# Graph-network stack on one core: job results of the pair stage added in twos by GpSimd ahead of the product with the identity

## Chip, core and metric

The kernel runs on one core of one Trainium2 chip. The metric is the time on the device in microseconds, lower is better; it is given as the median of several executions. TensorE (PE), its weight loads (PEld), VectorE (DVE), ScalarE (ACT), GpSimd (POOL) and the DMA queues (SyncE's is SP) work from queues of their own, in order, and wait for each other by semaphores.

## The reference

The reference is a stack of four graph layers over 2048 nodes, 8 batches and 64 features, each added to its input after a layer norm and a relu. The change lies in layer 0. Its part that matters here is this, with H the 2048 x 64 membership of nodes in hyperedges:

```python
all_he = beta[..., None] * h[:, None, :, :] + (1.0 - beta[..., None]) * agg[:, :, None, :]
all_he = jax.nn.elu(all_he)
...
coefs1 = jax.nn.softmax(logits2, axis=-1)
g = jnp.einsum('bne,benf->bnf', coefs1, all_he)
...
industry = jnp.einsum('nm,bmf->bnf', adj / deg, x @ W_ind)
```

For each node n, g sums over the hyperedges e that hold the node: elu of a mixture of the node's own features h and the hyperedge's features agg, weighted by coefs1. A node is in few hyperedges, so the kernel walks only over the pairs that exist. The industry term is a dense product with the adjacency matrix.

## The kernel before, in words

The kernel first tests on the chip whether the short form applies; with these inputs it does. The nodes are then ordered by the number of hyperedges that they are in, and cut into 16 tiles of 128 nodes. HELD (line 35) says for each j how many tiles hold nodes with more than j hyperedges. From it the class Pairs makes its list of jobs, (tile t, slot j): 57 in all, 12 for tile 0, 5 for tiles 1 and 2, 4 for tiles 3 to 5, 3 for tiles 6 to 9, 2 for tiles 10 to 14, and 1 for tile 15. Each job works on a block of 128 nodes x 512 values (8 batches x 64 features) in fp32.

The stage runs inside layer0_pairs. The dense product for the industry term, adj_product (line 321), loops over 4 column chunks and 16 row tiles: in each of these 64 steps it casts a block of the adjacency matrix on ScalarE (line 344) and issues 8 products, four with x_ind_hi and four with x_ind_lo, into four accumulators named pp. After each step it calls `after`, which runs one `Pairs.step()` and one piece of a side job, the naming of lists (line 2462). That side job has a VectorE comparison (L2469), 13 small products and a copy (L2478), each of them once in four steps. At the end of a chunk, VectorE multiplies the four accumulators into their place (L872).

One call of `Pairs.step()` works on four jobs in different states, as a software pipeline:

- job i: VectorE subtracts the gathered hyperedge row pa (in PSUM) from the node's row h (L2335), GpSimd scales the difference by beta (L2324, called from `scale`);
- job i-1: VectorE adds pa back (L2339), ScalarE makes exp(-relu(-d)) in two instructions (L2341, L2342);
- `gather(i + 1)`: two products of the selection matrix `pick` with agg_hi and agg_lo into a pa bank, of which there are two; if the job opens a new tile, first the fetch of a later tile by an indirect DMA on GpSimd's queue (L2268) and the tile's set-up (lines 2273 to 2309: `pick` on VectorE, small pb products, beta and coef);
- job i-2: VectorE forms y = max(d, 0) + e (L2347), GpSimd scales y by coef (L2324);
- job i-3: TensorE adds y to the tile's accumulator acc as a product with the identity (in fp32, two recorded matmuls each, `kern.mm` at line 177); at the tile's last job ScalarE writes the accumulator minus one (L2359), and a DMA on SyncE's queue stores it to g_rows.

d, e and y are rings of 8, 6 and 8 buffers; two further places of e hold the results for storing. All of TensorE's `kern.mm` products have line 177 in the profile. The stage behind it (`mix`) gathers g_rows by indirect DMAs (L890); none of these can start before all g_rows are stored.

The order in each engine's queue is not the order in which the program lists the instructions. A scheduler puts them in order when the kernel is built, from its own estimates of cost and readiness. It keeps dependences, but it may put VectorE's instructions of neighbouring jobs in another order than `step` lists them. Only three instructions in a later stage are told to keep program order.

Of the kernel before, what the change touches and what calls it, by code (L numbers as in the profile page):

```python
# [7 lines left out]
F = mybir.dt.float32  # L8
# [4 lines left out]
AF = mybir.ActivationFunctionType  # L13
# [6 lines left out]
P = 128  # L20
# [6 lines left out]
CW = 512  # L27
# [108 lines left out]
class Kernel:  # L136
# [184 lines left out]
    def adj_product(self, src, w, ps, done, each=None, first=None, after=None, bufs=4, step=2, casts=None):  # L321
# [4 lines left out]
        for ch in range(NC):  # L326
            out = [ps.tile([P, CW], F, name=f"pp{q}", tag=f"pp{q}") for q in range(NP)]
            if first is not None:
                first(ch, out)
            for g in range(NT // step):  # L330
                at = w.tile([P, step, CW], F, name="adj_t", bufs=bufs)
                nc.sync.dma_start(
                    at,
                    self.a["adjT"][g * step * P : (g + 1) * step * P, ch * CW : (ch + 1) * CW]
                    .rearrange("(t p) n -> p t n", p=P),
                )
                for i in range(step):
                    m = g * step + i
                    if each is not None:
                        each(ch, m, at[:, i])  # L340
                    moving = at[:, i]
                    if self.short:
                        moving = w.tile([P, CW], F12, name="adj_12", bufs=casts or bufs)
                        nc.scalar.copy(moving, at[:, i])
                    for j, part in enumerate(src.parts):
                        for q in range(NP):
                            self.mm(
                                out[q], self.exact(part(m)[:, q * P : (q + 1) * P]),
                                moving,
                                start=first is None and m == 0 and j == 0,  # L350
                                stop=m == NT - 1 and j == 1,
                            )
                    if after is not None:
                        after(ch, m, moving)
            done(ch, out)
# [1886 lines left out]
class Pairs:  # L2242
# [85 lines left out]
    def step(self):  # L2328

        nc, n, i = self.nc, len(self.jobs), self.i  # L2330
        self.i += 1
        if i < n:
            t, j = self.jobs[i]
            d = self.d[:, i % 8]
            nc.vector.tensor_sub(d, self.h[:, t % 4, : NB * D], self.pas[i])  # L2335
            self.scale(d, self.tiles[t][1][:, j])
        if 1 <= i < n + 1:
            d, e = self.d[:, (i - 1) % 8], self.e[:, (i - 1) % 6]
            nc.vector.tensor_add(d, d, self.pas.pop(i - 1))  # L2339

            nc.scalar.activation(e, d, AF.Relu, scale=-1.0)  # L2341
            nc.scalar.activation(e, e, AF.Exp, scale=-1.0)  # L2342
        self.gather(i + 1)
        if 2 <= i < n + 2:
            t, j = self.jobs[i - 2]
            d, e, y = self.d[:, (i - 2) % 8], self.e[:, (i - 2) % 6], self.y[:, (i - 2) % 8]
            nc.vector.scalar_tensor_tensor(y, d, 0.0, e, op0=OP.max, op1=OP.add)  # L2347
            self.scale(y, self.tiles[t][2][:, j])
        if 3 <= i < n + 3:
            t, j = self.jobs[i - 3]  # L2350
            if j == 0:
                self.accs[t] = self.ps.tile([P, CW], F, name="acc")
            self.kern.mm(
                self.accs[t], self.kern.ident, self.y[:, (i - 3) % 8], start=j == 0,
                stop=j == self.last[t],
            )
            if j == self.last[t]:
                g = self.e[:, 6 + t % 2]
                nc.scalar.activation(g, self.accs.pop(t), AF.Identity, bias=self.less)  # L2359
                nc.sync.dma_start(self.kern.g_rows[t * P : (t + 1) * P], g)  # L2360

    def end(self):
# [892 lines left out]
```

## Time and profile before

| | us |
|---|---|
| Median of 3 executions | 1943.07 (1941.38 to 1949.31) |
| Profiled execution, its own time | 1993.83 |
| Profiled execution, span | 1992.1 |
| of it, jobs of Pairs (first L2335 to last scaling) | about 214 to 438 |
| of it, end of the dense product (last L872) | 451 |
| TensorE clock granted, mean of the span | 0.918 of full speed |
| GpSimd, L2324, 57 by beta and 57 by coef, in the stage | 76.1 and 63.1 busy |
| ScalarE, casts of the adjacency blocks (L344), 64 | 0.608 each (median) |
| VectorE, naming comparison (L2469), 15 | 2.340 each (median), 1.878 at least |

A row of a group reads: line, engine, operation, output <- inputs by the program's names, shapes, count | busy us, mean ns of one | idle us of the engine just before them, and what ended most of it. The rings and other buffers in the big slots of SBUF all appear as `q`. A row of the waits reads: who waited <- for whom: us in total, times, longest. A row of the timeline reads: start, duration, engine, line, operation, and in brackets how long the engine had been idle before it and what ended that.

### The profile page before, as it was taken

To read this page: it belongs to the slowest core of one execution; us is meant where nothing else is said; L and a number is where in the kernel's file an instruction comes from. 1 tells how busy PE (TensorE), PEld (TensorE's weight loads), DVE (VectorE), ACT (ScalarE), POOL (GpSimd) and SP (SyncE) were. 2 spreads that over 40 slices of the span, in tenths; PEclk is the share of its full clock that TensorE was granted. 3 is DMA by queue.
4 is the path that set the end of the run, shared out by engine and by line. 5 is a ranking of instruction groups with operands and counts; after the bars stand their busy time and mean duration, and the time that the engine had idled before them with its cause. 6 is when DMAs were issued, how large, how long until landed. Compare 5 with 4: busy or idle time off the path is not lost. (4 is left out here: it accounts for less than half of the span.)

```text
span 1992.1 us, 22431 instructions
## 1 busy us (share of the span) xinstructions
PE 1714.6 (86%) x7094; PEld 979.9 (49%) x7098; DVE 1407.7 (71%) x2307; ACT 819.8 (41%) x1650; POOL 1047.7 (53%) x1007
## 2 busy tenths in 40 slices
PE   6888999898888788999999998788787899398884
PEld 2446766663234544444444443466576665244432
DVE  6888788764667787677766566889776675276774
ACT  5722445445566643212120101555555663185300
POOL 1101466668645645776755554563663440767760
PEclk8888999998897997999999998899799898698997
DMA  9641223336436753242220211687677674746555
GB/s 342 262 117 45 75 93 113 103 110 217 127 134 188 238 178 106 64 122 69 74 85 27 88 50 54 218 255 240 201 246 246 190 236 147 249 122 187 169 152 189
DMA packets 127226, 305.22 MB, mean 153 GB/s; under 512 B 29536, under 2 KB 33392, under 8 KB 121968
## 3 DMA queue, kind: packets, MB, share of 16 engines
q0 software_dynamic: 45328, 149.60, 24.8%
q1 hardware_dynamic: 79456, 149.81, 22.2%
q10 hardware_dynamic: 2304, 4.20, 0.6%
q8 instruction: 60, 0.98, 0.2%
q14 instruction: 78, 0.64, 0.1%
HBM read 240.40 MB, written 63.14 MB: 152 GB/s over the span
## 5 line engine op out<-in xcount | busy, mean ns | idle before, releaser
L2615 POOL DMA_INDIRECT raw<-sent,index x300 | 321.3, 1071 | 302.0 <-DVE part_lo L2633 124.6
L2632 ACT CAST part_hi<-raw 128x512 fp32r<-128x512 f32 x352 | 213.0, 619 | 336.0 <-PE acc L177 226.9
L2633 DVE TENSOR_TENSOR part_lo<-raw,part_hi 128x512 fp32r<-128x512 f32 x352 | 264.3, 775 | 113.5 <-ACT part_hi L2632 60.7
L177 PE MATMUL pk<-q,w 128*128 128x512 f32 (+1 forms) x768 | 307.6, 619 | 2.0 <-DVE q L1731 0.9
L1842 POOL TENSOR_TENSOR half<-half,y 128x512 f32<-128x512 f32 x180 | 230.9, 1312 | 117.2 <-DVE y L1835 116.5
L177 PE MATMUL acc<-q,ident 128*128 128x512 f32 x416 | 209.4, 629 | 42.1 <-issue 17.3
L177 PE MATMUL acc<-part_lo,weights 128*128 128x512 f32 x365 | 169.0, 465 | 38.0 <-DVE part_lo L2633 32.2
L177 PE MATMUL acc<-part_hi,weights 128*128 128x512 f32 x365 | 174.4, 481 | 28.4 <-issue 14.1
L177 PEld LDWEIGHTS pk<-q,w 128*128 128x128 f32 (+1 forms) x768 | 117.5, 193 | 156.3 <-issue 121.5
L1835 DVE SCALAR_TENSOR_TENSOR y<-pk,bias,q 128x512 f32<-128x512 f32 x210 | 148.0, 743 | 55.5 <-PE pk L177 37.5
L2944 POOL DMA_INDIRECT ring<-f_rows,near x121 | 138.0, 1141 | 70.2 <-issue 29.9
L177 PEld LDWEIGHTS acc<-q,ident 128*128 128x128 f32 x416 | 78.9, 200 | 121.5 <-issue 70.9
L177 PEld LDWEIGHTS acc<-part_lo,weights 128*128 128x128 f32 x365 | 74.1, 203 | 91.7 <-DVE part_lo L2633 61.4
L2324 POOL TENSOR_TENSOR q<-q,beta 128x512 f32<-128x512 f32 x57 | 76.1, 1337 | 71.3 <-DVE beta L2300 32.9
L177 PEld LDWEIGHTS acc<-part_hi,weights 128*128 128x128 f32 x365 | 73.2, 200 | 79.9 <-issue 49.6
L3015 DVE TENSOR_TENSOR q<-ring,e 128x1024 f32<-128x1024 f32 x58 | 70.1, 1218 | 30.2 <-remote 13.3
L177 PE MATMUL pp<-adj,x_ind_hi 128*128 128x512 f32 x256 | 90.5, 470 | 0.5 <-DVE q L872 0.3
L2601 ACT CAST hub_weights<-dense 128x384 fp32r<-128x384 uint8 x80 | 40.5, 511 | 88.5 <-PE acc L177 84.6
L292 DVE RECIPROCAL std<-std 128x512 f32<-128x512 f32 (+1 forms) x17 | 53.7, 3161 | 30.9 <-ACT std L291 30.9
L2324 POOL TENSOR_TENSOR q<-q,coef 128x512 f32<-128x512 f32 x57 | 63.1, 1108 | 21.2 <-DVE q L2347 16.9
L2532 POOL DMA_INDIRECT listed_raw<-in_adjT_dram,cell x60 | 63.4, 1057 | 16.5 <-issue 16.2
L177 PE MATMUL pp<-adj,x_ind_lo 128*128 128x512 f32 x256 | 72.0, 400 | 0.0
(504 smaller groups left out, 3485.9 us busy)
## 6 DMA issues: line engine op xcount, KB each, us to landing
rows<-in_adj_dram SPq DMA_DIRECT2D x16, 1024.0 KB
adj_t<-in_adjT_dram SPq DMA_DIRECT2D x64, 256.0 KB
own<-sent SPq DMA_DIRECT2D x52, 256.0 KB
raw<-sent SPq DMA_DIRECT2D x52, 256.0 KB
sent<-u SPq DMA_DIRECT2D x48, 256.0 KB
q<-x SPq DMA_DIRECT2D x9, 1024.0 KB
links<-squares POOLq DMA_DIRECT2D x16, 512.0 KB
sent<-q SPq DMA_DIRECT2D x32, 256.0 KB
```

The lines of the kernel that those rows point to most:

```text
L177: self.nc.tensor.matmul(out, lhsT, rhs, start=start, stop=stop)
L292: nc.vector.reciprocal(std, std)
L1835: nc.vector.scalar_tensor_tensor(y, pks[b, half], bias[:, b : b + 1], emb[:, b], op0=OP.add, op1=OP.mult,)
L1842: add.tensor_add(acc, acc, y)
L2324: self.nc.gpsimd.tensor_tensor(x, x, by.unsqueeze(2).to_broadcast([P, NB, D]), op=OP.mult)
L2532: self.kern.behind(nc.gpsimd.indirect_dma_start(raw[:, i], None, rows, bass.IndirectOffsetOnAxis(ap=self.cell[:, c + i : c + i + 1], axis= ...
L2601: self.nc.scalar.copy(to, self.lists.dense[:, :, i * P : (i + 1) * P])
L2615: self.nc.gpsimd.indirect_dma_start(raw, None, self.rows[:], bass.IndirectOffsetOnAxis(ap=self.lists.index[:, c : c + 1], axis=0),)
L2632: nc.scalar.copy(hi, raw)
L2633: nc.vector.tensor_sub(lo, raw, hi.bitcast(F))
L2944: self.nc.gpsimd.indirect_dma_start(to, None, self.kern.f_rows[:], bass.IndirectOffsetOnAxis(ap=index, axis=0))
L3015: nc.vector.tensor_tensor(y.rearrange("n i (b f) -> n i b f", b=NB), block[:, i : i + 2, : NB * D].rearrange("n i (b f) -> n i b f", b=NB) ...
```

## The change

The scaled results y of two neighbouring jobs of one tile are added on GpSimd: for an odd slot j, right after its scaling, y of slot j-1 is added to y of slot j, in place. TensorE then takes only the sums (odd j), and the last y of a tile with an odd number of jobs, into the accumulator. A tile with one or two jobs uses no accumulator: ScalarE reads its y, or its sum of two, directly from SBUF.

```diff
@@ -2346,17 +2346,22 @@
             d, e, y = self.d[:, (i - 2) % 8], self.e[:, (i - 2) % 6], self.y[:, (i - 2) % 8]
             nc.vector.scalar_tensor_tensor(y, d, 0.0, e, op0=OP.max, op1=OP.add)
             self.scale(y, self.tiles[t][2][:, j])
+            if j % 2:
+                nc.gpsimd.tensor_add(y, y, self.y[:, (i - 3) % 8])
         if 3 <= i < n + 3:
             t, j = self.jobs[i - 3]
-            if j == 0:
-                self.accs[t] = self.ps.tile([P, CW], F, name="acc")
-            self.kern.mm(
-                self.accs[t], self.kern.ident, self.y[:, (i - 3) % 8], start=j == 0,
-                stop=j == self.last[t],
-            )
-            if j == self.last[t]:
+            y, last = self.y[:, (i - 3) % 8], self.last[t]
+            if last > 1:
+                if j == 0:
+                    self.accs[t] = self.ps.tile([P, CW], F, name="acc")
+                if j % 2 or j == last:
+                    self.kern.mm(
+                        self.accs[t], self.kern.ident, y, start=j < 2, stop=j == last
+                    )
+            if j == last:
                 g = self.e[:, 6 + t % 2]
-                nc.scalar.activation(g, self.accs.pop(t), AF.Identity, bias=self.less)
+                total = self.accs.pop(t) if last > 1 else y
+                nc.scalar.activation(g, total, AF.Identity, bias=self.less)
                 nc.sync.dma_start(self.kern.g_rows[t * P : (t + 1) * P], g)
```

## Prediction

> **What bounds the kernel now.** I read the page first (engine shares and the 40 slices), then the stage's stretch alone (busy time by window), then who waits for whom in it, then the groups of instructions, and last the timeline of single steps. The page says that TensorE is the busiest engine, but that is a mean over all stages:
>
> ```profile
> span 1992.1 us, 22431 instructions
> PE 1714.6 (86%) x7094; PEld 979.9 (49%) x7098; DVE 1407.7 (71%) x2307; ACT 819.8 (41%) x1650; POOL 1047.7 (53%) x1007
> ```
>
> The jobs of the class Pairs run from the first subtraction at 214.2 us to the last scaling just before 438 us. The stretch 214 to 438 us, columns PE, PEld, DVE, ACT, POOL busy:
>
> ```profile
> 214.00:438.00 224.00, 207.67 (x968) 146.07 (x967) 182.31 (x340) 111.65 (x202) 151.35 (x126) 0.99 0.30 101
> ```
>
> 57 jobs in 224 us are 3.93 us each. TensorE shows 207.7, but ends of matmuls are modelled, so I count it from starts below. Now the waits from 213 to 446 us (total, times, longest):
>
> ```profile
> ...
> POOL q L2324 <- DVE q L2335: 29.4, 26, 2.5
> DVE q L2339 <- POOL q L2324: 28.9, 32, 1.2
> ACT adj L344 <- PE pp L177: 26.3, 20, 3.4
> ...
> PE pa L177 <- DVE q L2339: 12.7, 14, 2.4
> ...
> DVE q L2347 <- ACT q L2342: 9.3, 11, 1.4
> ...
> DVE q L2335 <- PE pa L177: 0.4, 1, 0.4
> ```
>
> What to see: VectorE is busy 182.3 us and waits 28.9 us for GpSimd and 9.3 us for ScalarE: 220.5 of 224 us. Its subtraction L2335, the only instruction of a job that needs TensorE first, waited for TensorE 0.4 us in all. So the queue that sets the pace is VectorE's, with its round trips to GpSimd; TensorE is nearly full beside it, and itself waits 12.7 us for VectorE. One round trip in the timeline:
>
> ```profile
> 308.21 0.68 DVE L2347 SCALAR_TENSOR_TENSOR q<-q,q 128x512 f32<-128x512 f32 x1
> 308.43 1.36 POOL L2324 TENSOR_TENSOR q<-q,beta 128x512 f32<-128x512 f32 x1 [2.49 <-DVE q L2335]
> ...
> 309.75 1.04 POOL L2324 TENSOR_TENSOR q<-q,coef 128x512 f32<-128x512 f32 x1
> 309.82 0.69 DVE L2339 TENSOR_TENSOR q<-q,pa 128x512 f32<-128x512 f32 x1 [0.94 <-POOL q L2324]
> ```
>
> The subtraction of a job is followed by L2347 of the job before, and then VectorE stands 0.94 us until the scaling of the same job is done. The program lists the next subtraction ahead of that addition; the built order puts it after. The scheduler that orders the queues at build time chose so.
>
> TensorE's price of one product with the identity, from its weight loads where nothing else is in between:
>
> ```profile
> 440.70 0.42 PEld L177 LDWEIGHTS acc<-q,ident 128*128 128x128 f32 x2
> 441.35 0.19 PEld L177 LDWEIGHTS pp<-adj,x_ind_hi 128*128 128x128 f32 x1 [0.24 <-issue]
> 441.78 0.66 PEld L177 LDWEIGHTS pp<-adj,x_ind_hi 128*128 128x128 f32 x3 [0.24 <-issue]
> ```
>
> The first load ends and the product starts at 440.92; the second product of the next group starts to load at 441.78: 0.86 us for the two passes of one product. A step without additions costs TensorE 0.93 for four products of adj with x_ind_hi, as much for x_ind_lo, 0.47 for pa and 0.86 for the identity, 3.2 us (from the first pa product at 305.93 to that of the next step at 309.12 the timeline has 3.19). With 57 x 3.2, 14 us for the pb products (114 at 0.126) and 4 us for naming it is 200 of 224 us.
>
> Durations that the change needs (the first row is of another stage, the others of 215 to 437 us):
>
> ```profile
> L1842 POOL TENSOR_TENSOR half<-half,y 128x512 f32<-128x512 f32 x180 | 230.9, 1312 | 117.2 <-DVE y L1835 116.5
> ...
> L2324 POOL TENSOR_TENSOR q<-q,beta 128x512 f32<-128x512 f32 x57 | 76.1, 1337 | 71.3 <-DVE beta L2300 32.9 <-DVE q L2335 29.4 <-DVE beta L2294 4.9
> ...
> L2324 POOL TENSOR_TENSOR q<-q,coef 128x512 f32<-128x512 f32 x57 | 63.1, 1108 | 21.2 <-DVE q L2347 16.9 <-DVE found L2478 1.5 <-DVE beta L2294 1.1
> ...
> L2347 DVE SCALAR_TENSOR_TENSOR q<-q,q 128x512 f32<-128x512 f32 x57 | 44.2, 776 | 9.3 <-ACT q L2342 9.3
> ```
>
> **What the Trainium skill says.** "SBUF — State Buffer", section "Who interferes with whom": a VectorE instruction with two SBUF inputs and a GpSimd instruction that reads SBUF exclude each other for their whole length. The trace agrees: the scaling takes 1.04 us alone, 1.36 where L2347 runs beside it, and 2.69 beside the 1.88 us of L2469; L2335 and L2339, with one input in PSUM, don't lengthen it. "GPSIMD Engine Reference", section "Elementwise — side-by-side cycle accounting": an fp32 add of two tensors with 2048 elements takes 4497 ns on GpSimd, so an estimate of 1.12 us for 512. The trace has 1.27 us as the median of L1842 (1.25 to 1.73); that is used.
>
> **The change part by part.**
> (a) Products removed. Tile 0 has 12 jobs, tiles 1 and 2 have 5, 3 to 5 have 4, 6 to 9 have 3, 10 to 14 have 2, tile 15 has 1. Removed: 6 + 4 + 6 + 4 + 10 + 1 = 31 of 57; 31 x 0.86 = 26.7 us of TensorE, leaving 174 of 224. None of it lies on VectorE's queue. It reaches VectorE only through ScalarE: the cast L344 waits 26.3 us for TensorE, with L2341 and L2342 queued behind it. Of VectorE's 9.3 us of waiting for ScalarE I take 5 as gone (0 to 9.3). The six tiles without the product read y in SBUF at L2359; no ScalarE instruction is added, and its wait for TensorE (2.1 us) and TensorE's wait for the accumulator's bank (2.0) shrink beside other work: nothing.
> (b) Additions. 6 + 4 + 6 + 4 + 5 = 25 on GpSimd, 25 x 1.27 = 31.8 us (to 43 at 1.73): 151 becomes 183 of 224. Each stands behind a scaling by coef and ahead of the next job's scaling by beta, and of a fetch (L2268) where a tile begins. GpSimd idles in these queues 71.3 + 21.2 less 23.6 before the first job = 68.9 us, 1.2 us a job in two gaps of 0.6. An addition fills the 0.6 that it finds and pushes the next scaling by 0.67: 25 x 0.67 = 16.8 us. Only where VectorE waits for that scaling (32 of 57) is it seen: 9.4 us (0 to 16.8). TensorE's product waits for the addition instead of the scaling, with the next pp products queued behind it; three steps of slack lie between, and GpSimd cost this product 3.3 us before: nothing.
> (c) The shared port. An addition that has started holds L2347 back. Bounds: none, as L2347 finds another moment, to 25 x 1.27 = 32 us if each meets it fully. L2347's own excess over its 0.68 median was 57 x 0.09 = 5 us beside 114 scalings; 25 longer instructions at about that rate give 1.5, and I take 3.
> (d) Order of the queues. The built order follows estimates of the scheduler that this trace doesn't hold. With 31 products gone, pa of the next job is ready 0.86 us earlier in 31 of 57 steps, and the scaling later: both move the next L2335 (0.68 us) ahead of L2339, where the program lists it, into a wait of 0.9. If all 32 waits take one, it is 32 x 0.6 = 19 us; bounds: nothing, and the whole 28.9. I take 19.
>
> **Sum.** -5 + 9.4 + 3 - 19 = -11.6 us. The profiled execution takes 1993.83 us (span 1992.1 and 1.7 around it); it becomes 1982. It is 50.8 us (2.6%) above the median of 1943.07, so I carry the difference over: 1943.07 - 11.6 = 1931.5. Behind the stage nothing changes: the stage's last products and the gather L890 that waits for g_rows both come earlier by it. Next to be late are GpSimd (183) and VectorE (182), so the stage can't fall much below 195 us.
>
> **Rivals.** (1) The order moves in half of the waits only: -9.5 in place of -19, sum about -2: 1941. For it: VectorE bursts (L2469, the tile's set-up) split the steps anyway. Against: GpSimd has only 0.6 us per gap, so the scheduler must move something. (2) Slower: the order stays, and every round trip through GpSimd gets longer. No gain in (d), ScalarE still -5, additions 9.4, L2347 held by half its length behind each addition, 25 x 0.34 = 8.5: sum +13, 1956. For it: VectorE never waits for TensorE, so TensorE's relief alone is worth nothing. It decides from the point where VectorE's waits and stretching, 38 us now, pass 48 us. Against: GpSimd still idles a fifth of the stretch. That the change doesn't do what it says can be excluded: the counts follow from HELD.
>
> **Chances.** A difference of 0.5% (9.7 us) is about what a measurement of this kernel can tell from no change. Forecast 0.44, rival (1) 0.33, rival (2) 0.23; they give faster 0.44, same 0.33, slower 0.23. Low end: all waits but the additions' 9.4 go, 38 - 9.4 = 29, to 1915; high end: 1954, just short of the middle of rival (2), leaves some 2 in 10 out on both sides together.
>
> **What would show it.** Right: L2335 directly ahead of L2339 with its wait for GpSimd under 15 us in all; 26 products with the identity; 25 additions at 1.27 to 1.4 us; the stretch near 212 us. Wrong: L2339's wait over 35 us, or L2347's mean over 900 ns, with the stretch at 230 us or more; or a difference that lies behind the stage, in other queues that the scheduler ordered anew.

## The result, and the profile after

The changed kernel takes 1954.9 us (median of 8 executions, 1947.15 to 1961.02), the kernel before 1944.37 us (8 executions, 1941.38 to 1949.31). The ratio is 1.0051 (95% interval 1.0032 to 1.0070): 10 us slower, where 11.6 us faster was forecast. A second measurement gave 1.0053 (1.0030 to 1.0077). The rival that ended slower had 1956.

The profiled execution of before is not a good partner for the whole span: its 1993.83 us fit a chip on which the kernel before has a median of 1987 us (below). The stage itself is a better one. Two kernels were profiled on that slower chip and on a faster one: the stage of the first took 215.0 and 215.1 us, that of the second 235.5 and 232.3. So the stage is compared directly, but a difference of less than some 3 us between chips says nothing; times are compared only as ratios within a chip. These are three of the stage's instructions in the two profiles (count, duration min/median/max in ns, start of the first and of the last); first before, then after:

```profile
L2335 DVE TENSOR_TENSOR q<-q,pa x57: 633/677/687, 214.2 to 431.3; 128x512 f32<-128x512 f32 x57
...
L2324 POOL TENSOR_TENSOR q<-q,coef x57: 1037/1044/2687, 222.3 to 436.8; 128x512 f32<-128x512 f32 x57
...
L890 POOL DMA_INDIRECT q<-g_rows,order x16: 946/949/1091, 445.6 to 486.3; - x16
```

```profile
L2335 DVE TENSOR_TENSOR q<-q,pa x57: 672/676/690, 217.5 to 444.2; 128x512 f32<-128x512 f32 x57
...
L2324 POOL TENSOR_TENSOR q<-q,coef x57: 1036/1043/2690, 225.7 to 454.7; 128x512 f32<-128x512 f32 x57
...
L890 POOL DMA_INDIRECT q<-g_rows,order x16: 942/946/1308, 459.7 to 504.7; - x16
```

From the first subtraction to the start of the last scaling the jobs take 436.8 - 214.2 = 222.6 us before and 454.7 - 217.5 = 237.2 us after: 14.6 us more. The gather that opens the next stage starts 231.4 us after the first subtraction before, 242.2 us after: 10.8 us more, which is the whole loss. The two numbers differ by 3.8 us, which the change gives back at the very end of the stage. Before, the product of the last job (tile 15) stood behind the dense product in TensorE's queue, and ScalarE could read the result only 5.2 us after the last scaling had started, at 436.8 us. Now ScalarE reads y itself, 1.1 us after the last scaling has started, at 454.7 us. First before, then after:

```profile
441.98 0.69 ACT L2359 ACTIVATE q<-acc,less 128x512 f32<-128x512 f32 x1 [0.24 <-PE acc L177]
```

```profile
455.76 0.72 ACT L2364 ACTIVATE q<-q,less 128x512 f32<-128x512 f32 x1 [1.27 <-POOL q L2324]
```

The stretch of the jobs (PE, PEld, DVE, ACT, POOL busy), 239 us in place of 224:

```profile
217.00:456.00 239.00, 205.26 (x962) 148.90 (x961) 197.32 (x349) 117.44 (x206) 194.25 (x151) 0.94 0.30 95
```

GpSimd goes from 151 to 194 us. VectorE, which has the same jobs as before, goes from 182.3 to 197.3. Its waits in the same stretch:

```profile
DVE q L2339 <- POOL q L2324: 28.5, 27, 1.9
DVE q L2335 <- PE pa L177: 9.2, 11, 2.3
DVE beta L2299 <- ACT beta L2298: 1.9, 1, 1.9
DVE beta L2294 <- PE pb L177: 1.1, 4, 0.3
DVE found L2483 <- PE pa L177: 0.4, 1, 0.4
DVE q L2347 <- ACT q L2342: 0.3, 1, 0.3
```

They sum to 41.4 us; before they were 40.0 (28.9 + 9.3 and 1.8 of small ones). Against the kernel before, the waits changed their names, not their sum: ScalarE's 9.3 went, TensorE's 9.2 came, GpSimd's stayed. What grew by 15.0 us is the time in which VectorE counts as busy. The groups say with what:

```profile
L2347 DVE SCALAR_TENSOR_TENSOR q<-q,q 128x512 f32<-128x512 f32 x57 | 50.9, 893 | 0.3 <-ACT q L2342 0.3
...
L2474 DVE TENSOR_TENSOR q<-short_line,low 128x1664 bf16<-128x1664 bf16 x14 | 34.8, 2483 | 0.0
```

```profile
L2324 POOL TENSOR_TENSOR q<-q,beta 128x512 f32<-128x512 f32 x57 | 74.8, 1314 | 52.3 <-DVE beta L2300 26.6 <-DVE q L2335 24.4 <-DVE coef L2306 1.3
L2324 POOL TENSOR_TENSOR q<-q,coef 128x512 f32<-128x512 f32 x57 | 73.1, 1282 | 9.8 <-DVE q L2347 5.6 <-DVE found L2483 2.6 <-DVE beta L2294 1.4
L2350 POOL TENSOR_TENSOR q<-q 128x512 f32<-128x512 f32 x25 | 35.0, 1400 | 2.0
```

On VectorE, the same 57 instructions L2347 take 6.7 us more than before (44.2), the naming comparison (L2469 before, L2474 now) 2.4 more (32.4), and 3.9 us are the naming's last instructions, which came behind the jobs before and lie among them now. On GpSimd, the 57 scalings by coef take 10.0 more (63.1), and the added instructions 1.40 us each, 35.0 in all. These differences mix the additions with a new order of VectorE's queue (below), which the run without additions separates. How a single addition lengthens what stands beside it is seen in one step of the timeline after:

```profile
429.88 1.29 POOL L2350 TENSOR_TENSOR q<-q 128x512 f32<-128x512 f32 x1
...
430.72 0.99 DVE L2347 SCALAR_TENSOR_TENSOR q<-q,q 128x512 f32<-128x512 f32 x1
...
431.12 1.50 POOL L2324 TENSOR_TENSOR q<-q,beta 128x512 f32<-128x512 f32 x1
...
431.63 2.73 DVE L2474 TENSOR_TENSOR q<-short_line,low 128x1664 bf16<-128x1664 bf16 x1
```

L2347 has two inputs in SBUF. It starts 0.45 us ahead of the addition's end and takes 0.99 us in place of 0.68. The scaling behind the addition then meets L2347 and takes 1.50 in place of 1.04, and the naming comparison meets the scaling and takes 2.73 in place of 1.88. This is what the Trainium skill's "SBUF — State Buffer" says in "Who interferes with whom", one holding the other for its whole length; in this step all of it is booked as busy time, and none as a wait.

TensorE has a new wait, too, which the prediction had put at nothing:

```profile
PEld acc L177 <- POOL q L2350: 19.8, 14, 3.3
...
PE acc L177 <- POOL q L2350: 14.4, 11, 2.8
```

The two rows are in part the same moments (the longest stand, before 383.6 us, is in both), so they are not to be added up.

One thing beside the queues differs, too. The clock that TensorE was granted over this stretch has a mean of 0.94, where the kernel before had 0.99 (0.96 without the additions, 0.97 with the additions alone). No run holds it constant, so how much of VectorE's wait for TensorE comes from it is not shown. It is not what makes the additions dear: where they stand alone (below), VectorE waits only 0.8 us for pa.

Last, the order of VectorE's queue: in how many of the 57 jobs the next job's subtraction L2335 stands ahead of the job's addition L2339.

| kernel | L2335 ahead |
|---|---|
| before | 7 |
| changed | 26 |
| as the program lists them | 56 |

So the move that step (d) of the prediction counted on did happen, for 19 jobs more where it took 32, and L2339's wait for GpSimd was 28.5 us all the same.

### The profile page after: what moved, and what is told of

The parts are those of the page before. It is cut to its first block, busy times and chain, and to the rows that moved or that the text cites. A ratio compares the mean times of both kernels' runs of the same rounds, so it can differ in the third digit from the quotient of the medians.

```text
span 1956.9 us, 22263 instructions
## 1 busy us (share of the span) xinstructions
PE 1691.4 (86%) x7036; PEld 966.5 (49%) x7036; DVE 1418.5 (72%) x2307; ACT 822.9 (42%) x1650; POOL 1084.4 (55%) x1032
## 5 line engine op out<-in xcount | busy, mean ns | idle before, releaser
L2620 POOL DMA_INDIRECT raw<-sent,index x300 | 317.0, 1057 | 275.5 <-DVE part_lo L2638 111.5
L177 PE MATMUL acc<-q,ident 128*128 128x512 f32 x354 | 173.6, 624 | 40.3 <-DVE q L3039 18.1
L177 PEld LDWEIGHTS acc<-q,ident 128*128 128x128 f32 x354 | 64.1, 195 | 115.5 <-issue 41.9
L177 PE MATMUL pp<-adj,x_ind_hi 128*128 128x512 f32 x256 | 85.5, 445 | 0.0
L177 PE MATMUL pp<-adj,x_ind_lo 128*128 128x512 f32 x256 | 79.1, 421 | 0.0
L2324 POOL TENSOR_TENSOR q<-q,coef 128x512 f32<-128x512 f32 x57 | 73.1, 1282 | 9.8 <-DVE q L2347 5.6
```

The source lines that it names most:

```text
L177: self.nc.tensor.matmul(out, lhsT, rhs, start=start, stop=stop)
L2324: self.nc.gpsimd.tensor_tensor(x, x, by.unsqueeze(2).to_broadcast([P, NB, D]), op=OP.mult)
L2620: self.nc.gpsimd.indirect_dma_start(raw, None, self.rows[:], bass.IndirectOffsetOnAxis(ap=self.lists.index[:, c : c + 1], axis=0),)
```

## The experiments

Three theories. **A**: the additions cost what they take of GpSimd's queue and of the SBUF port that it shares with VectorE. **B**: TensorE, in order, stands before a product whose addition is not done, with the dense product behind it. **C**: the scheduler's new order costs by itself. "Jobs" below is the stretch from the first L2335 to the start of the last scaling by coef: 222.6 us before, 237.2 in the changed kernel. Each ratio is to the kernel before on the same chip.

**No additions.** An edit of the changed kernel:

```diff
-            if j % 2:
-                nc.gpsimd.tensor_add(y, y, self.y[:, (i - 3) % 8])
```

> The changed kernel without the 25 GpSimd additions; the products of the even slots stay out, so their results are missing from g. Queues: VectorE's subtraction ahead of the previous job's addition in 25 of 57 steps, as in the changed kernel (26). Theory A (the additions take GpSimd's time and the port that it shares with VectorE): the whole loss goes and TensorE's relief shows, 1930 to 1938, VectorE's wait for GpSimd under 20 us in all. Theory B (TensorE stands behind the addition in its queue): the same range, as the addition is gone too. Theory C (the new order of the queues itself costs): no faster than the kernel before, 1944 to 1955.

1932.87 us, ratio 0.9958 (0.9940 to 0.9975): 8 us faster than before. Jobs 221.0 us, gather at 226.0 us (5.4 less than before). Theory C falls, since this kernel has the new order. Against it the changed kernel's jobs are 237.2 - 221.0 = 16.2 us longer: this is what the additions cost there.

```profile
L2347 DVE SCALAR_TENSOR_TENSOR q<-q,q 128x512 f32<-128x512 f32 x57 | 52.2, 915 | 0.3 <-ACT q L2342 0.3
L2339 DVE TENSOR_TENSOR q<-q,pa 128x512 f32<-128x512 f32 x57 | 38.8, 681 | 17.2 <-POOL q L2324 17.1
```

L2347 is no shorter here than in the changed kernel (50.9 us), so its growth there comes with the new order: of the 31 that are longer than 0.75 us, each begins while a scaling is under way. In the changed kernel there are 31 of them, too, 11 that begin during an addition and 20 during a scaling. What the additions do to VectorE in the changed kernel is mostly waiting: 28.5 us for GpSimd in place of 17.1, and 9.2 us for TensorE's pa in place of 6.4. The selection matrix (L2280) takes 3.8 us more and the naming comparison 2.4, and one wait in a tile's set-up is 3.9 us shorter.

**Additions alone.** An edit of the kernel before:

```diff
             self.scale(y, self.tiles[t][2][:, j])
+            if j % 2:
+                nc.gpsimd.tensor_add(self.y[:, (i + 1) % 8], y, self.y[:, (i - 3) % 8])
```

> The kernel before with the 25 additions issued at the same places, their results written to a free place of the ring and not used; all 57 products stay, and no product waits for an addition. VectorE's queue has the order of before (subtraction ahead of the addition in 7 of 57). Theory A: slower by 8 to 16 us, 1952 to 1960, VectorE's L2347 and the naming comparison longer as in the changed kernel, its wait for GpSimd at 35 us or more. Theory B and C: within 4 us of the kernel before, 1941 to 1948.

1967.75 us, ratio 1.0108 (1.0077 to 1.0139): 21 us slower, more than theory A expected. Jobs 244.4 us, 21.8 more than before, with VectorE's queue in the order of before. Both marks of theory A are there:

```profile
L2350 POOL TENSOR_TENSOR q<-q 128x512 f32<-128x512 f32 x25 | 37.2, 1487 | 2.0
...
L2347 DVE SCALAR_TENSOR_TENSOR q<-q,q 128x512 f32<-128x512 f32 x57 | 52.2, 918 | 9.5 <-ACT q L2342 9.5
L2339 DVE TENSOR_TENSOR q<-q,pa 128x512 f32<-128x512 f32 x57 | 39.0, 683 | 36.5 <-POOL q L2324 36.5
```

L2339 waits 36.5 us for GpSimd (28.9 before), L2347 is busy 8.0 us longer, and the set-up's L2280 and L2299 together 5.1. The naming comparison, which was to be longer too, is not (32.2). So 37 us of GpSimd's time, in an engine that stood idle for 69 us of the stretch before, lengthened the stage by 22 us.

**GpSimd's time without the port.** The same places, filled with GpSimd instructions that write SBUF and read nothing:

```diff
             self.scale(y, self.tiles[t][2][:, j])
+            if j % 2:
+                for _ in range(3):
+                    self.kern.behind(nc.gpsimd.memset(self.blank, 0.0))
```

> The kernel before with 25 groups of three GpSimd fills of a spare 128 x 384 block (about 1.25 us a group, written and not read), where the run with the additions alone had an addition. Nothing of the result changes. If the cost of the additions is GpSimd's time in its queue: as dear as the additions alone, 1958 to 1968. If it is VectorE held at the shared port by an instruction that reads SBUF: half of it or less, 1944 to 1954, with L2347's mean near the 776 ns of the kernel before.

1953.27 us, ratio 1.0061 (1.0041 to 1.0082). Jobs 235.0 us, 12.4 more than before, in place of 21.8.

```profile
L2352 POOL MEMSET blank<- 128x384 f32 x75 | 31.5, 419 | 2.5
...
L2348 DVE SCALAR_TENSOR_TENSOR q<-q,q 128x512 f32<-128x512 f32 x57 | 45.9, 806 | 8.8 <-ACT q L2343 8.7
L2340 DVE TENSOR_TENSOR q<-q,pa 128x512 f32<-128x512 f32 x57 | 38.9, 683 | 36.7 <-POOL q L2325 36.7
```

The wait for GpSimd is 36.7 us, as with the additions; what is missing is most of L2347's lengthening (806 ns, 776 before, 918 with the additions). So some 12 of the 22 us are GpSimd's queue, and some 9 come with the reading of SBUF. The split is rough: the fills are 5.7 us shorter in all, and in the first tile some stand one place off. The time lies within the range that was expected if VectorE is held, and L2347 near its length of before; but the fills cost more than half of what the additions cost, so both theories have a share.

**The product one step later**, so that TensorE meets a finished addition:

```diff
-        if 3 <= i < n + 3:
-            t, j = self.jobs[i - 3]
-            y, last = self.y[:, (i - 3) % 8], self.last[t]
+        if 4 <= i < n + 4:
+            t, j = self.jobs[i - 4]
+            y, last = self.y[:, (i - 4) % 8], self.last[t]
...
-        while self.i < len(self.jobs) + 3:
+        while self.i < len(self.jobs) + 4:
```

> The changed kernel with the product (and the store of a tile) one step later, so that TensorE meets an addition that is done. Theory B: TensorE's wait for the addition (34 us in the changed kernel) falls under 8, VectorE's wait for TensorE (9 us) goes, and the time comes to 1940 to 1947. Theory A: these waits go but the additions still hold GpSimd and the port; 1951 to 1958.

1954.31 us, ratio 1.0055 (1.0034 to 1.0075): nothing gained. The wait of TensorE's products for the additions falls from 14.4 to 1.5 us, that of their weight loads from 19.8 to 3.1 (the 34 us of the expectation are 14.4 and 19.8 added up), and VectorE's for pa from 9.2 to 4.5. L2347 rises to 54.8 us busy, 3.9 above the changed kernel. Jobs 235.6 us, 1.6 less than in the changed kernel, and the gather at 243.2 us, 1.0 more. In the scheduler's own order theory B explains no part of the loss that can be seen in the time.

**The listed order alone**, step (d) of the prediction by itself. An edit of the kernel before, with no addition and all products:

```diff
-            nc.vector.tensor_add(d, d, self.pas.pop(i - 1))
+            added = nc.vector.tensor_add(d, d, self.pas.pop(i - 1))
+            if i < n:
+                self.kern.behind(added)
```

> The kernel before with one order imposed: VectorE's L2339 of a job is queued behind L2335 of the next job, as the program lists them (56 of 57 steps, 7 in the kernel before); nothing else. It tests step (d) of the prediction alone. If that step's mechanism holds: VectorE's wait for GpSimd falls from 29 us to under 12 and the time to 1925 to 1936. Theory C (a new order costs): 1948 or more, with VectorE now waiting for TensorE's pa by 10 us or more.

> The kernel before with the listed order once more, beside the two others on the same chip: 1931 to 1938, faster than the kernel before by 0.2 to 0.6%.

1934.15 us, ratio 0.9958 (0.9941 to 0.9976); the second time, on the slower chip, 1976.08 us beside 1987.3, ratio 0.9945 (0.9924 to 0.9966). Jobs 215.1 and 215.0 us. It is 8 to 11 us faster than the kernel before, and so the fastest version here that computes everything. The first time lies in the range that was expected if the mechanism of step (d) holds. But the wait that it takes away was 28.9 us, and it takes it away wholly:

```profile
L2349 DVE SCALAR_TENSOR_TENSOR q<-q,q 128x512 f32<-128x512 f32 x57 | 66.7, 1171 | 4.1 <-ACT q L2344 4.0
L2335 DVE TENSOR_TENSOR q<-q,pa 128x512 f32<-128x512 f32 x57 | 38.6, 677 | 9.3 <-PE pa L177 9.0
L2339 DVE TENSOR_TENSOR q<-q,pa 128x512 f32<-128x512 f32 x57 | 38.5, 676 | 0.0
```

L2339 waits for nothing any more. L2349 (L2347 before) is busy for 66.7 us in place of 44.2, and the subtraction waits 9.0 us for TensorE in place of 0.4. One place of its timeline shows why: with the subtraction moved ahead, the scaling by beta is under way when L2349's turn comes.

```profile
299.83 1.04 POOL L2324 TENSOR_TENSOR q<-q,beta 128x512 f32<-128x512 f32 x1
300.08 1.34 DVE L2349 SCALAR_TENSOR_TENSOR q<-q,q 128x512 f32<-128x512 f32 x1
```

VectorE waited for GpSimd's result before; now it is held at the port by the same GpSimd instruction. This place stands for most: 41 of the 57 L2349 are longer than 0.75 us and begin while a scaling by beta is under way, and they make up 22.4 us of what all are above 0.68 us each, 28 us. Before, there were 4, with 1.0 us. Of the 28.9 us, 22.5 come back as L2349's length.

**TensorE's relief with the order held.** The kernel without additions, with the listed order:

> The changed kernel without additions (even slots' results missing from g) and with L2339 queued behind the next job's L2335 in 56 of 57 steps. Against the kernel before with this order alone it differs only by 31 products less: TensorE's relief with the order held. If VectorE, GpSimd and their port set the pace (theory A): no more than 4 us below that kernel, 1930 to 1937. If TensorE's 9 us of holding up VectorE there are what is left: 1922 to 1929.

1971.26 us on the slower chip, ratio 0.9928 (0.9908 to 0.9949), beside 0.9945 for the listed order alone in the same runs. Jobs 213.3 against 215.0 us. So 31 products less, 26.7 us of TensorE, are worth about 2 us of the jobs when the order doesn't move; the two intervals overlap. VectorE's wait for pa did not fall with it (10.9 us). TensorE's products stood 12.4 us for scalings that were not done, against 3.3 us with the order alone.

**The changed kernel in the listed order**, without and with the later product:

> The changed kernel with VectorE's L2339 queued behind the next job's L2335 in 56 of 57 steps (26 in the changed kernel). Theory A: the additions cost their 16 us here too, so it lies above the listed order alone (1934): 1944 to 1953, VectorE's wait for GpSimd under 15 us but L2347 over 1200 ns in the mean. If the remaining half of the order was what the changed kernel lacked, the prediction's step (d): 1926 to 1936.

> The changed kernel with that same order and with the product one step later. In the changed kernel with the order alone TensorE stood 31 us before products whose addition was not done, and VectorE 21 us for TensorE. Theory A: these waits fall under 8 and 8, and the time comes down a few us, to 1948 to 1955, since the additions' own cost stays. Theory B (the in-order TensorE queue is what costs there): 1934 to 1944.

> The changed kernel with the listed order. Theory A, and no part of TensorE's standing: the same as the changed kernel with that order and the product one step later. Theory B: 0.4% or more above it, as it was when the two ran on different chips (1.0063 and 0.9999 of the kernel before).

> The changed kernel with the listed order and the product one step later. If the difference to the run without the later product was the chip's: 1.004 to 1.008 of the kernel before. If TensorE's standing in front of unfinished additions is a part of the loss: 0.998 to 1.002.

> The changed kernel beside the two others on one chip: 0.3 to 0.7% above the kernel before under either theory.

| kernel | ratio, first | ratio, again | jobs, us |
|---|---|---|---|
| changed | 1.0051 (1.0032 to 1.0070) | 1.0053 (1.0030 to 1.0077) | 237.2, 237.3 |
| changed, listed order | 1.0063 (1.0043 to 1.0082) | 1.0076 (1.0048 to 1.0105) | 245.2, 245.2 |
| the same, product later | 0.9999 (0.9980 to 1.0018) | 1.0032 (1.0017 to 1.0047) | 235.5, 232.3 |

The first time the third row ran on the slower chip; "again" are all three on one. Step (d)'s full order does not rescue the change: the jobs get 8 us longer than in the changed kernel, and its first time, 1958.16 us, lies above both expectations. In this order TensorE stands before unfinished additions far longer, and VectorE after it:

```profile
PE acc L177 <- POOL q L2352: 31.2, 20, 2.8
```

```profile
DVE q L2335 <- PE pa L177: 21.0, 22, 3.0
```

With the product one step later these fall to 16.3 and 12.8 us in the second measurement (both were expected under 8), and the jobs by 10 to 13. Here theory B is a part of it, some 0.4% of the time, although the two intervals all but touch (1.0048 and 1.0047), and 1.0032 lies between the two ranges that were expected. Even so the additions leave their cost: 232.3 or 235.5 us of jobs against 213.3 without them.

**Additions on VectorE.** An edit of the changed kernel:

```diff
-                nc.gpsimd.tensor_add(y, y, self.y[:, (i - 3) % 8])
+                nc.vector.tensor_add(y, y, self.y[:, (i - 3) % 8])
```

> The changed kernel with the 25 additions on VectorE in place of GpSimd. If VectorE's own queue sets the pace: 25 x 0.68 = 17 us more of it, less what the shorter use of the shared port and the absent GpSimd time give back; with the 5 us that the stage gained without additions, 1946 to 1953. If it is GpSimd's queue that made the additions dear, they are cheap here: 1936 to 1942.

1949.26 us, ratio 1.0021 (1.0008 to 1.0035): slower than before, less so than on GpSimd, and in the range that was expected if VectorE's own queue sets the pace. 25 additions take 20.5 us of VectorE's queue, which then waits 13.0 us in front of them for the scalings. Jobs 236.9 us, no shorter than in the changed kernel, and the gather at 242.5 us, 11.1 later than before, where the whole kernel loses only 4 us. The profiled execution took 1955.8 us, 6.5 above the median, so its stage may be longer than usual; this was not settled.

**Short tiles only.** Tiles 10 to 15 as in the changed kernel (5 additions, 11 products less), the others as before:

```diff
-            if j % 2:
+            if j % 2 and self.last[t] == 1:
...
-                if j % 2 or j == last:
-                    self.kern.mm(
-                        self.accs[t], self.kern.ident, y, start=j < 2, stop=j == last
-                    )
+                self.kern.mm(
+                    self.accs[t], self.kern.ident, y, start=j == 0, stop=j == last
+                )
```

> Only tiles 10 to 15 changed (5 additions, 11 products less); tiles 0 to 9 as in the kernel before. Order of VectorE's queue as before (9 of 57). At 16 to 21 us for 25 additions, 5 cost 3 to 4 us; the relief of 11 products gives 0 to 2: 1942 to 1947. If the end of the stage is what is long in the changed kernel (additions that ScalarE and the store wait for), 1949 or more.

1944.04 us, ratio 0.9993 (0.9972 to 1.0015): no difference. Jobs 227.4 us, 4.8 more than before (5 of 25 additions, at 21.8 us for all, would be 4.4), but the gather starts only 1.0 us later: 3.8 us are given back behind the last scaling, as in the changed kernel. So the end of the stage is not where the changed kernel loses, but where it gains.

## Why the prediction was wrong, step by step

**What bounds the stage** was read rightly: VectorE's queue with its round trips to GpSimd, and not TensorE. TensorE's relief with the order held is worth about 2 us of jobs.

**(a) Relief, -5 us through ScalarE.** VectorE's wait for ScalarE did go, 9.3 to 0.3 us, in the changed kernel and without additions alike. But a wait for TensorE's pa came with it (9.2 and 6.4 us), which no step of the prediction had. And the tiles without a product, put at nothing, are worth 3.8 us: the last tile's result no longer passes through TensorE's queue.

**(b) and (c), +9.4 and +3 us.** The mechanisms were right, the sizes too small: 12.4 us were forecast; the additions cost 16.2 us of jobs in the changed kernel and 21.8 us in the order of before. In the order of before GpSimd's queue alone cost some 12 (for 9.4), what comes with reading SBUF some 9 (for 3), L2347 being 8.0 us longer. Step (c) priced L2347's share of the holding up only. It left out that a held L2347 ends later and holds the next scaling, which holds the naming comparison: the step at 429.88 us shows all three. How much of the loss is due to such chains was not measured. The addition itself was priced at 1.27 us and took 1.40. And (b) put the product's wait for the addition at nothing with "three steps of slack": TensorE's products stood there for 14.4 us. In the scheduler's order that cost nothing that the later product could give back; in the listed order it cost some 0.4%.

**(d) Order, -19 us.** This is the step that failed, and that turned the sign. The prediction took it that the order would move in all 32 waits, and that each moved subtraction would fill 0.6 us of one. It moved in 26 of 57 jobs against 7. And the price was wrong even where it moves everywhere: the listed order alone took 28.9 us of waiting and gave 7.5 us of jobs. A VectorE that doesn't wait for GpSimd's scaling runs beside it, and then L2347, with two SBUF inputs, is held by it, 22.5 us in all. With half of the order the account is the same: without additions, the wait for GpSimd fell by 11.8 us, L2347 grew by 8.0 and the wait for pa by 6.0, and relief and order together made the jobs 1.6 us shorter, less than two chips can differ by. The prediction named this exclusion and used it for the additions, but not for the two scalings per job that were there already.

**The sum** forecast -11.6 us: -24 for relief and order, +12.4 for additions. In jobs it was -1.6 (the run without additions) and +16.2, together +14.6; at the gather -5.4 and +16.2, together +10.8, and 0.51% of 1944 us is 10 us. Rival (2) had the sign and nearly the number (1956). Its point of decision was passed as well: VectorE's waits and stretching grew by some 12 us (1.4 of waits, and 15.0 busy less the naming's 3.9), where it asked for 10. But its premise, that the order stays, was not what happened, so the nearness of its number is in part luck.

What stays open: why VectorE's wait for TensorE's pa is 8.5 to 21 us in every kernel with the listed order and 2.7 to 9.3 in those with the scheduler's new one, against 0.4 before, with or without the 31 products. TensorE's products stand longer there for a scaling or an addition (1.5 to 32 us, 0.5 before), and the clock granted is mostly lower (0.93 to 0.98, but 0.99 with the listed order alone); no run separates the two. Open is, too, where the kernel with additions on VectorE gets back what its stage loses.

## What to carry to other kernels

A wait on one engine for another is worth only what its removal leaves: ask which resource the two will share once they run side by side, here the SBUF port of VectorE and GpSimd, and count the holders that are there already, not only the new ones. Idle time of an engine in the loop is not free room: 37 us put into 69 us of GpSimd's idle time lengthened the loop by 22, in part because that idle time lay where VectorE waited for that engine's next result. And look at the mean length of unchanged instructions: contention for a port stands in the busy column, where no table of waits shows it. Compare it with a run that leaves out the suspected instruction, not only with the kernel before: L2347 was as long without the additions as with them.

## What was not expected of the hardware

The same kernel before had medians of 1941.8 to 1944.4 us in some measurements and 1987.3 us in another, on another chip, over 2% apart; the two other kernels that were measured on both kinds of chip were 2.0 and 2.2% slower there. Their stage was nearly as long on both (jobs 215.1 and 215.0 us, 232.3 and 235.5 us). Twenty-five groups of GpSimd fills that read nothing, 31.5 us in all, left L2347 at a mean of 806 ns, where additions of 37.2 us in all made it 918.
